# Two-layer cross-attention on one core: where the softmax portions stand beside small projections, which engine copies the fifth and sixth transposes, and when the last weight sums are made

## The chip, the cores and the metric

The kernel runs on one core of a Trainium2 chip. Its time is the device time of one execution in microseconds, median of several runs. The engines that matter here are TensorE (PE in the profile, with its weight loads PEld), VectorE (DVE), ScalarE (ACT), GpSimd (POOL) and SyncE (SP), which issues most loads. Everything is float32.

## The reference

Two cross-attention layers follow each other. There are 8 batches, 100 query rows, 640 channels in 20 heads of 32, and 722 context rows of 1024 channels: the first 77 are "text", the other 645 are "ip". Cut to what matters:

```python
# layer 0
q = split(x @ Wq.T)
out = attend(q, text @ Wk.T, text @ Wv.T) + attend(q, ip @ Wk_ip.T, ip @ Wv_ip.T)
x = out @ Wo.T + bo + x
# layer 1
q = x @ Wq; k_text = text @ Wk; scale = 1 / sqrt(32)
text_out = attend(q, k_text, text @ Wv)
text_probs = softmax(q @ k_text.T * scale)          # over all 640 channels at once
sem = ((text_probs @ text) @ ip.T) * scale          # one row of 645 per query
ip_probs = softmax(scores_ip + 0.5 * sem) * mask
x = (text_out + ip_probs @ ip_v) @ Wout + bout + x
```

`attend` is softmax(q k^T / sqrt(32)) v, per head. The text and the ip part have softmaxes of their own, whose results are added.

## The kernel before

A *unit* u from 0 to 15 is a layer and a batch (u // 8, u % 8); two units make a *pair*. An attention *step* (u, c) is one unit and one chunk c of 128 channels, that is 4 heads. There are 80 steps in `ORDER`: by unit and chunk, except that the last pair goes by groups of chunks, (14,0) (14,2) (15,0) (15,2) (14,1) (14,3) (15,1) (15,3) (14,4) (15,4).

Two streams of work are woven into each other on TensorE.

*Production* makes keys and values of the context, for the pair after the one in attention, and writes them to DRAM, from where each step loads its part. It uses a scheme with seven products in place of eight (`seven`): sums of weights and sums of context blocks are formed first, and results are put together as they leave PSUM. Each task is one product of about 2 us. For the last pair the weights are cut anew: `last_weights` loads them, and `weight_sums` makes four sums, L134 to L137. They are put into the task list of the pair before by `insert` (L1090), at a mark and so many tasks ahead of it: `("k 4", 1, ...)` is one task before the end of that pair's last key products. The first products of the last pair (`psvk`, L736 and L741) read these sums and the block sums `sl` (L232, L233).

*Attention* takes a step in this order. `scores` (L939) computes the logits of one step in two parts (columns 0 to 511, then 512 to 721), takes the maxima on VectorE, and puts the rest of the softmax into a list `later`, as *portions*: `exponentials` (L975, and L993 and L994 with the text part), then `factors` with `scaled_rest(False)` (L997 to L1001, L1015), then two of `scaled` (L1007, two heads each; the first with `scaled_rest(True)`, L1011). `emit(n)` (L931) issues the first n portions. `transposes` (L1036) turns the softmax of the step *before* into six blocks: four transposes into one PSUM tile `pspt` (L1043), then a copy to SBUF, on ScalarE (L1048) or VectorE (L1050). `values` (L1052) multiplies them with v into `pv` and copies the result to `hs` (L1069). Before the first transposes of a step everything in `later` is issued, and so it is before the first scores of a step.

Beside these there are *small* pieces of work, handed out by `small_work(n)`: `out_piece` (output projection, L863, and its addition on VectorE, L868), `q_piece` (queries of layer 1, L882, copied by ScalarE, L886), the `sem_` functions (`sem_text` L836 and L838; `sem_logits` L810 with L815 to L818; `sem_transpose` L823, L825; `sem_scores` L845, L846), and `last_out` (L915). Small pieces, transposes and values all take their PSUM tile from one pool, `ps_pt`, with two buffers: whoever asks waits until the tile two or so before has been read out. In layer 0 output pieces come in steps with c = 1 of even u, in layer 1 the sem pieces of the next unit in steps with c = 3 and 4.

`between(n, a, b, small)` (L1255) weaves one quarter of a step. It runs production tasks up to a point in the plan, sees to it that two things without production between them get a task there (`apart`), and then runs each small piece. Each production task with TensorE work issues one portion before it (`next_task`, L1234), and so does each small piece (L1262).

The order on TensorE, VectorE and ScalarE is fixed: `manual_schedule` (L1225) keeps these three engines in the order in which the program issues. Loads on SP and stores on POOL are placed by the framework. So a line that is issued earlier stands earlier in its engine's queue, whether or not its input is there.

Of the kernel before, what the change touches and what calls it, by code (L numbers as in the profile page):

```python
# [38 lines left out]
PAIRS = [(2 * i, 2 * i + 1) for i in range(NU // 2)]  # L39
# [5 lines left out]
def two_layer_xattn(  # L45
# [47 lines left out]
    def load_quarters(kind, src, n):  # L93

        rows = src.rearrange("(k p) n -> p k n", p=P)
        for i in range(2):
            for j in range(2):
                load_quarter(kind, rows, n, i, j)
# [28 lines left out]
    def weight_sums(kind, n, engines=None):  # L127

        b11, b12, b21, b22 = (W[kind, f"b{x}"] for x in ("11", "12", "21", "22"))
        t2, t3, t4 = (weight_tile(f"w{kind}t{x}", n) for x in (2, 3, 4))  # L130
        W[kind, "t1"], W[kind, "t2"], W[kind, "t3"], W[kind, "t4"] = b12, t2, t3, t4
        first, then = engines or (nc.vector, nc.vector)
        parts = [
            lambda: first.tensor_tensor(t3, b22, b12, ALU.subtract),  # L134
            lambda: first.tensor_tensor(t2, t3, b11, ALU.add),
            lambda: then.tensor_tensor(b12, b12, b11, ALU.subtract),
            lambda: then.tensor_tensor(t4, b21, t2, ALU.subtract),  # L137
        ]
        if engines is None:
            return parts  # L140
        for f in parts:
            f()

    def load_wv(src):
        load_quarters("v", src, HC)
# [5 lines left out]
    def load_wk4(src):  # L151
        W["k", 4] = wpool.tile([P, NCC, P], F32, tag="wk4", name="wk4")
        nc.sync.dma_start(W["k", 4], src.rearrange("(k p) n -> p k n", p=P)[:, :, 4 * P :])
# [299 lines left out]
    def load_q(u):  # L453
        l, b = divmod(u, B)
        t = tpool.tile([P, NC_, S], F32, tag="q", name=f"q_{u}")
        nc.sync.dma_start(t, q_d[l][b // 2][:, b % 2])
        qs_[u] = t
# [471 lines left out]
    later = []  # L929

    def emit(n):  # L931
        for _ in range(n):
            later.pop(0)[1]()
# [102 lines left out]
    def transposes(u, c, j, at_end=False):  # L1036
        if j == 0:
            emit(len(later))
            pts[u, c] = one.tile([P, 6, 4 * S], F32, tag="pt", name=f"pt_{u}_{c}")
        rows = P if j < 5 else NTAIL  # L1040
        ps = ps_pt.tile([P, 512], F32, tag="pt", name=f"pspt_{u}_{c}_{j}")
        for i in range(4):
            nc.tensor.transpose(  # L1043
                ps[:rows, i * S : (i + 1) * S], pr[u, c][:, i, j * P : j * P + rows], ident[:S, :S]
            )
        dst, src = pts[u, c][:rows, j, :], ps[:rows, : 4 * S]
        if j % 3 == 2 or at_end and j == 0:
            nc.scalar.copy(dst, src)  # L1048
        else:
            nc.vector.tensor_copy(dst, src)  # L1050
# [23 lines left out]
    def production():  # L1074

        plan = []
        all_tasks = [pair_tasks(PAIRS[i]) for i in range(1, len(PAIRS) - 1)]
        parts = {}

        def sums_later(kind, n, i):  # L1080
            if kind not in parts:
                parts[kind] = weight_sums(kind, n)
            parts[kind][i]()
            if i == 3:
                del parts[kind]

        def asked(kind, n):
            return [(0.0, lambda i=i: sums_later(kind, n, i)) for i in range(4)]

        def insert(i, *what):  # L1090

            marks = pair_marks[PAIRS[i]]
            for mark, back, tasks in sorted(what, key=lambda w: -(marks[w[0]] - w[1])):
                at = marks[mark] - back
                all_tasks[i - 1][at:at] = tasks


        v, k = asked("v", HC), asked("k", 2 * P)
        insert(
            B // 2 - 1,  # L1100
            ("fifth 4", 0, [(0.0, lambda: load_wk4(wki[1]))]),
            ("v 4", 0, [(0.0, lambda: load_wv(wvi[1]))]),
            ("k 4", 1, v[:1]),
            ("k 4", 0, v[1:2] + [(0.0, lambda: load_quarters("k", wki[1], 2 * P))]),
        )
        insert(
            B // 2,
            ("fifth 0", 1, v[2:3]), ("fifth 0", 0, v[3:]),
            ("fifth 1", 1, k[:1]), ("fifth 1", 0, k[1:2]), ("v 1", 6, k[2:3]), ("v 1", 4, k[3:]),
        )  # L1110

        v_last = asked("v", 2 * P)
        insert(len(PAIRS) - 2, ("v 4", 0, [(0.0, last_weights)]), ("k 4", 1, v_last[:1]), ("k 4", 0, v_last[1:2]))
        for i, tasks in enumerate(all_tasks):
            plan.append((10 * i - AHEAD, 10 * i + 10 - AHEAD, tasks))
        n = 5 * LAST[0]
        every = list(range(NB))
        visits = [(j, lambda j, xs, i, r=r: two_chunks(r, j, xs, i)) for r in range(2) for j in every]
        for kinds, js in (("kv", every[:2]), ("k", every[2:]), ("v", every[2:])):
            visits += [(j, lambda j, xs, i, kinds=kinds: fifth_chunk(kinds, j, xs, i)) for j in js]  # L1120
        lists = last_visits(visits)

        lists[0][5:5] = v_last[2:3]
        lists[0][7:7] = v_last[3:]
        for a, b, tasks in (
            (n - 10 - AHEAD, n + 2.9, lists[: 2 * NB]),
            (n + 2.9, n + 6.9, lists[2 * NB : 3 * NB]),
            (n + 6.9, n + 8.95, lists[3 * NB :]),
        ):
            plan.append((a, b, [t for one_list in tasks for t in one_list]))  # L1130
        return [task for a, b, tasks in plan for task in spread(a, b, tasks)]
# [93 lines left out]
    with tc.manual_schedule(engines={mybir.EngineType.PE, mybir.EngineType.DVE, mybir.EngineType.Activation}):  # L1225
        for _, f in pair_tasks(PAIRS[0]):
            f()
        load_q(0)
        load_vt(0)
        load_k(0, 0)  # L1230
        todo = production()
        done = [0]

        def next_task():  # L1234

            if todo[done[0]][0] and later:
                emit(1)
            todo[done[0]][2]()
            done[0] += 1

        def make(until):
            while done[0] < len(todo) and todo[done[0]][1] < until:
                next_task()

        mark = [0]

        def apart(until):

            while done[0] < len(todo) and todo[done[0]][1] < until and not any(
                t for t, _, _ in todo[mark[0] : done[0]]  # L1250
            ):
                next_task()
            mark[0] = done[0]

        def between(n, a, b, small):  # L1255

            mark[0] = done[0]
            near = 0.4 if n < NC_ * LAST[0] + 6 else 0.1
            for i, (_, f) in enumerate(small):
                make(n + a + (b - a) * (i + 1) / (len(small) + 1))  # L1260
                apart(n + b + near)
                if later:  # L1262
                    emit(1)
                f()
            make(n + b)
            apart(n + b + near)

        make(0.0)
        last = None
        for n, (u, c) in enumerate(ORDER):  # L1270
            at = small_work(n)
            loads(n)
            scores(u, c, 0)
            if n == len(ORDER) - 1:
                load_v(*last)
                load_v(u, c)
            between(n, 0.0, 0.4, at[0])
            if last:
                transposes(*last, 0)
                transposes(*last, 1)  # L1280
            between(n, 0.4, 0.6, at[1])
            if last:
                transposes(*last, 2)
                transposes(*last, 3)
            scores(u, c, 1)
            if n == NC_ * LAST[0] - 1:
                load_q(LAST[1])
            between(n, 0.6, 0.8, at[2])
            if n < len(ORDER) - 2:
                load_v(u, c)  # L1290
            if n + 1 < len(ORDER):
                load_k(*ORDER[n + 1])
            if last:
                transposes(*last, 4)
                transposes(*last, 5)
            between(n, 0.8, 1.0, at[3])
            if last:
                values(*last)
            last = (u, c)
        last_out(0, [NC_ - 1])  # L1300
        for j in range(6):
            transposes(*last, j, at_end=True)
        last_out_add(0)
        values(*last)
        last_out(1, [NC_ - 1])
        last_out_add(1)
# [46 lines left out]
```

## Time and profile before

| what | value |
|---|---|
| median of 3 runs | 2088.91 us (2087.19 to 2090.65) |
| the profiled execution | 2091.22 us, its span 2089.5 us |
| mean granted TensorE clock | 0.995 |
| copies of transposes on VectorE (L1050) | 319, mean 569 ns |
| copies of transposes on ScalarE (L1048) | 161, mean 489 ns |
| VectorE, sum over the span | 1096.1 us |
| ScalarE, sum over the span | 791.4 us |

The span runs from the first instruction to the last; the profiled execution's own time lies 1.7 us above it. TensorE's share of busy time counts modelled ends of matmuls, and a matmul at half clock is busy for longer. In the busy digits of the page TensorE is at 9 tenths in all slices but the last; VectorE and ScalarE are about half busy over the attention. Engines other than TensorE have idle time nearly everywhere, and their busy sums say little: what counts is when a result is there that TensorE waits for.

The lines of a timeline are: start, length, engine, line, operation, output and inputs, shapes, count, and in brackets the idle time of the engine before it with what ended it.

### The profile page before, as it was taken

What the parts mean: (1) busy time and instruction counts of PE and PEld (TensorE: products, weight loads), DVE (VectorE), ACT (ScalarE), POOL (GpSimd) and SP (SyncE); (2) the same over time, 40 slices, a digit from 0 to 9 for tenths busy, and PEclk for the clock granted to TensorE, in tenths of its full rate; (3) what the DMA queues carried; (4) which work ended last, traced back from release to release, by engine and by line L of the source; (5) the groups of instructions that cost most, each with busy time, mean ns of one, the idle gap of its engine ahead of it and who ended that gap; (6) DMA issues with size and microseconds to landing.
All of it is one profiled execution on the core that took longest, in us unless ns stands there. A gap on an engine that the chain in (4) does not pass through costs nothing. (4 is left out here: it accounts for less than half of the span.)

```text
span 2089.5 us, 38492 instructions
## 1 busy us (share of the span) xinstructions
PE 2051.0 (98%) x15122; PEld 1585.3 (76%) x15122; DVE 1096.1 (52%) x2989; ACT 791.4 (38%) x2271; POOL 310.3 (15%) x445
## 2 busy tenths in 40 slices
PE   9999999999999999999999999999999999999998
PEld 8676768677768677776778777787868778888787
DVE  2211222455564555555574655555565556777676
ACT  1001000234343443344333434344444444555576
POOL 3212311111111111010110111101111011111120
PEclk9999999999999999999999999999999999999999
DMA  9545314232424443262634433352425253544382
GB/s 327 157 130 168 93 57 114 84 100 83 120 79 134 119 116 85 87 171 74 175 111 142 120 107 93 91 160 81 122 73 159 75 164 103 161 127 129 110 226 65
DMA packets 302547, 255.38 MB, mean 122 GB/s; under 512 B 46686, under 2 KB 271378, under 8 KB 302366
## 3 DMA queue, kind: packets, MB, share of 16 engines
q1 hardware_dynamic: 280590, 184.48, 32.3%
q0 software_dynamic: 21776, 68.44, 9.5%
q8 instruction: 119, 1.95, 0.4%
q14 instruction: 62, 0.51, 0.1%
HBM read 183.93 MB, written 68.93 MB: 121 GB/s over the span
## 5 line engine op out<-in xcount | busy, mean ns | idle before, releaser
L1050 DVE COPY pt<-pspt 128x400 f32<-128x400 f32 x319 | 175.5, 569 | 135.8 <-PE pspt L1043 133.0
L975 ACT ACTIVATE p<-sc,st 100x512 f32<-100x512 f32 (+1 forms) x320 | 166.0, 531 | 208.2 <-DVE st L961 134.6
L1043 PE MATMUL pspt<-ident,p 100*128 100x100 f32 (+1 forms) x1920 | 214.1, 251 | 24.2 <-DVE res L868 10.9
L1043 PEld LDWEIGHTS pspt<-ident,p 100*128 100x128 f32 (+1 forms) x1920 | 188.7, 137 | 62.8 <-DVE res L868 12.9
L975 ACT ACTIVATE p<-p,st 100x512 f32<-100x512 f32 (+1 forms) x320 | 176.7, 554 | 125.7 <-DVE st L967 125.7
L1007 ACT ACTIVATE p<-p,st 100x512 f32<-100x512 f32 x320 | 208.1, 714 | 42.4 <-DVE st L1001 42.3
L597 PE MATMUL psv_a<-wv,x 128*128 128x397 f32 (+1 forms) x560 | 184.9, 472 | 0.0
L646 POOL DMA_DIRECT2D k_d<-ko x140 | 99.9, 717 | 528.8 <-DVE ko L219 478.6
L597 PE MATMUL psv_d<-wv,s 128*128 128x320 f32 (+1 forms) x560 | 174.9, 455 | 0.0
L1048 ACT COPY pt<-pspt 128x400 f32<-128x400 f32 (+1 forms) x161 | 78.7, 489 | 253.9 <-PE pspt L1043 252.5
L967 DVE CUSTOM_DVE_ANT_0 p<-sc,sem 100x512 f32<-100x512 f32 (+1 forms) x320 | 138.8, 491 | 24.3 <-PE sc L952 24.2
L597 PEld LDWEIGHTS psv_a<-wv,x 128*128 128x128 f32 x560 | 103.5, 189 | 62.1 <-issue 8.1
L597 PEld LDWEIGHTS psv_d<-wv,s 128*128 128x128 f32 x560 | 103.4, 190 | 57.5 <-issue 5.5
L961 DVE TENSOR_REDUCE st<-sc 100x2 f32<-100x1024 f32 (+1 forms) x160 | 125.3, 825 | 30.7 <-PE sc L952 30.7
L952 PE MATMUL sc<-k,q 32*100 32x210 f32 (+1 forms) x1280 | 138.9, 503 | 0.0
L625 PE MATMUL psk_d<-s,wk 128*128 128x256 f32 (+1 forms) x672 | 137.3, 350 | 0.0
L625 PE MATMUL psk_a<-x,wk 128*128 128x256 f32 (+1 forms) x672 | 135.5, 346 | 0.0
L612 POOL DMA_DIRECT2D v_d<-vo x70 | 38.5, 550 | 635.6 <-DVE gst L587 311.5
L563 PE MATMUL psk<-x,wk 128*128 128x256 f32 (+1 forms) x560 | 132.1, 383 | 0.0
L625 PEld LDWEIGHTS psk_a<-x,wk 128*128 128x128 f32 x672 | 109.2, 189 | 20.4 <-issue 6.0
L563 PEld LDWEIGHTS psk<-x,wk 128*128 128x128 f32 x560 | 102.5, 188 | 26.1 <-issue 9.9
L625 PEld LDWEIGHTS psk_d<-s,wk 128*128 128x128 f32 x672 | 108.5, 189 | 17.9 <-issue 5.2
(209 smaller groups left out, 3268.2 us busy)
## 6 DMA issues: line engine op xcount, KB each, us to landing
x<-ip_t SPq DMA_DIRECT2D x84, 512.0 KB
k<-k_d SPq DMA_DIRECT2D x80, 322.5 KB
v<-v_d SPq DMA_DIRECT2D x80, 320.0 KB
v_d<-vo POOLq DMA_DIRECT2D x70, 320.0 KB, 2.5
k_d<-ko POOLq DMA_DIRECT2D x112, 128.0 KB, 4.2
x<-ip_t SPq DMA_DIRECT2D x22, 532.0 KB
o<-wo SPq DMA_DIRECT2D x35, 320.0 KB
q<-wq SPq DMA_DIRECT2D x20, 320.0 KB
```

The source lines that it names most:

```text
L563: nc.tensor.matmul(ps[:, : 2 * n], lhsT=W["k", 4][:, k, :], rhs=x_all[:, at[j], :, k, :n], start=(k == 0), stop=(k == NCC - 1),)
L597: nc.tensor.matmul(ps[:, :m], lhsT=tokens(k)[:, :P], rhs=w[:, k, :], start=(k == 0 and not go_on), stop=(k == HK - 1), skip_group_check=True,)
L625: nc.tensor.matmul(ps[:, i * m : (i + 1) * m], lhsT=W["k", WHICH[which]][:, k, r * P : (r + 1) * P], rhs=tokens(k), start=(i == 0 and k == ...
L646: nc.gpsimd.dma_start(dst[:, :, r], ko[0][:, h, :, i, p0 : p0 + n])
L952: nc.tensor.matmul(scs[i // 2][:S, i % 2, : k1 - k0], lhsT=qs_[u][rows, c, :], rhs=ks[u, c][rows, k0:k1], start=True, stop=True)
L961: nc.vector.tensor_reduce(st[:, part, 2 * h : 2 * h + 2], scs[h][:S, :, :n], AX.X, ALU.max, negate=True)
L967: nc.vector.tensor_tensor_reduce(out=p[:, i, k0 : k0 + n], in0=scs[h][:S, i % 2, :n], in1=sems[u][:, k0 : k0 + n], scale=-1.0, scalar=3.0e ...
L975: nc.scalar.activation(dst, dst if l else scs[h][:S, i % 2, :n], AF.Exp, bias=st[:, part, i : i + 1], scale=-1.0 if l else 1.0, accum_out= ...
L1007: nc.scalar.activation(p[:, i, :KA], p[:, i, :KA], AF.Copy, scale=mul[:, 0, i : i + 1])
L1043: nc.tensor.transpose(ps[:rows, i * S : (i + 1) * S], pr[u, c][:, i, j * P : j * P + rows], ident[:S, :S])
L1048: nc.scalar.copy(dst, src)
L1050: nc.vector.tensor_copy(dst, src)
```

## The change

Three edits. In `between` a small piece no longer issues a portion before itself; portions are issued beside production tasks alone, and where everything is issued. In `transposes` the copies on ScalarE are those of j = 2 and 4, before of j = 2 and 5 (in the last step also j = 0, as before); j = 4 has 128 rows and j = 5 has 82. And the first two weight sums of the last pair are issued one task earlier each: two tasks and one task before the end of the key products, before one and none.

```diff
         dst, src = pts[u, c][:rows, j, :], ps[:rows, : 4 * S]
-        if j % 3 == 2 or at_end and j == 0:
+        if j in (2, 4) or at_end and j == 0:
             nc.scalar.copy(dst, src)
         else:
             nc.vector.tensor_copy(dst, src)
...
         v_last = asked("v", 2 * P)
-        insert(len(PAIRS) - 2, ("v 4", 0, [(0.0, last_weights)]), ("k 4", 1, v_last[:1]), ("k 4", 0, v_last[1:2]))
+        insert(len(PAIRS) - 2, ("v 4", 0, [(0.0, last_weights)]), ("k 4", 2, v_last[:1]), ("k 4", 1, v_last[1:2]))
...
             for i, (_, f) in enumerate(small):
                 make(n + a + (b - a) * (i + 1) / (len(small) + 1))
                 apart(n + b + near)
-                if later:
-                    emit(1)
                 f()
```

In the programs as built, TensorE's order of matmuls is the same before and after. On VectorE and ScalarE some sixty instructions or groups change places, all within their step; on SP five loads of one step change places; POOL's order is the same.

## The prediction

> **What bounds the kernel now.** I read the page's busy line first, then the waits of TensorE alone, then the timeline around its longest waits, then the windows view for the clock.
>
> ```profile
> PE 2051.0 (98%) x15122; PEld 1585.3 (76%) x15122; DVE 1096.1 (52%) x2989; ACT 791.4 (38%) x2271; POOL 310.3 (15%) x445
> ...
> PE pspt L1043 <- DVE res L868: 10.9, 11, 1.9
> PE pspt L1043 <- ACT tp L816: 7.3, 6, 2.7
> PE psq L275 <- DMA wq<-wq: 4.7, 1, 4.7
> PE pspt L1043 <- DVE pt L1050: 2.6, 2, 2.3
> PE psvk_b L736 <- DVE sl L233: 2.5, 1, 2.5
> ```
>
> TensorE is busy 2051.0 of 2089.5 us. Its order of matmuls is the same in both programs as built, so the change can act in only two ways: on the 38 us in which TensorE is not busy, and on the clock it runs at. The waits (line, releaser: us in total, times, longest) name what it waits for: a transposed portion pspt that finds no free PSUM buffer, because the buffer's last user, a small projection (L868) or a logit row (L816), has not been read out. The reader sees how in the timeline of step (11,3):
>
> ```profile
> 1739.40 0.71 DVE L1015 TENSOR_TENSOR p<-p,st 100x532 f32<-100x532 f32 x1
> 1740.03 0.23 DVE L815 TENSOR_REDUCE sst<-psm 100x1 f32<-100x77 f32 x1
> 1740.29 0.33 ACT L816 ACTIVATE tp<-psm,sst 100x77 f32<-100x77 f32 x1 [2.97 <-DVE sst L815]
> ...
> 1740.76 0.54 PE L1043 MATMUL pspt<-ident,p 100*82 100x100 f32 x4 [1.41 <-ACT tp L816]
> ...
> 1741.12 1.22 DVE L135 TENSOR_TENSOR wvt<-wvt,wv 128x1024 f32<-128x1024 f32 x1
> 1742.25 0.69 DVE L232 TENSOR_TENSOR sl<-x 128x512 f32<-128x512 f32 x1
> 1742.97 0.69 DVE L233 TENSOR_TENSOR sl<-sl,x 128x512 f32<-128x512 f32 x1
> 1743.81 0.46 PE L736 MATMUL psvk_b<-wvt,sl 128*128 128x128 f32 x2 [2.50 <-DVE sl L233]
> ```
>
> The logits were done at 1737.2, but L815 stands on VectorE behind the softmax portion L997 to L1015, which itself waited for ScalarE. Last, the windows view (PE, PEld, DVE, ACT, POOL busy, then the granted clock):
>
> ```profile
> 652.02:655.44 3.42, 1.51 (x12) 1.21 (x11) 2.81 (x9) 0.70 (x2) 0.57 (x1) 1.00 0.60 173
> 655.44:658.85 3.41, 3.41 (x11) 3.05 (x10) 0.42 (x1) 2.25 (x4) 0.53 (x1) 0.50 0.00 0
> 1744.29:1747.70 3.41, 3.41 (x30) 3.19 (x33) 1.27 (x3) 0.00 (x0) 0.00 (x0) 0.50 0.00 0
> 1833.04:1839.87 6.83, 6.03 (x64) 5.80 (x68) 2.02 (x7) 3.36 (x7) 0.91 (x2) 0.50 0.41 97
> 1952.50:1959.33 6.83, 5.97 (x60) 3.80 (x64) 3.27 (x12) 4.38 (x10) 0.00 (x0) 0.50 0.07 24
> ```
>
> After four of the long waits TensorE runs at half clock for 3.4 or 6.8 us, and counts as busy there. A wait can cost more than its own length.
>
> **What the Trainium skill says.** "TensorE: Matmul & The Clock Gate", Part 1, says that TensorE's clock goes to half after an idle window of about 3.4 us, counted in free-running windows. The windows above agree on half rate and the 3413 ns step. On the trigger the trace differs: a wait of 1.91 us inside one window (652.25 to 654.16) was enough, while equal waits at 892 and 1127, which by that 3413 ns grid straddle a boundary, were followed by full clock. The same page ("Engine queue depths") says that VectorE and ScalarE take their queues strictly in order; the timeline agrees, L815 waits though its input is there.
>
> **The change, part by part.** Times are of before's execution.
>
> *No portion beside small projections, waits of L868.* In steps (2,1), (4,1), (6,1), (8,1), (12,1) and (14,2) the fourth L868 moves ahead of L997 to L1015. It then starts 0.2 us after its matmuls, as it does elsewhere, where the wait left is 0.18 us. So 3 x (1.91 - 0.18) + (1.47 - 0.18) + (1.41 - 0.18) + (1.39 - 0.18) = 8.9 us.
>
> *Waits of L816.* In the p = 3 steps L815 moves ahead of the portion, and L816 ahead of L1007. The waits at 1284 (1.14), 1517 (0.70) and 1919 (0.89) go fully. At 1833 (2.71) L815 still follows L731 and L213, which ends at 1831.30: L815 0.23, L816 0.33 and two handovers of 0.1 give 1831.9 against a natural 1831.13, so 0.75 stays and 1.96 goes. Sum 4.7 us.
>
> *Two products sooner.* L134 (1.22) now stands before the evacuation L219 at 1733.11, before which VectorE idles 1.96 us, so it is hidden if its weights have landed. They were issued by 1718.1, and the DMA share falls to near nothing between 1724 and 1727; if they had not, SP's queue would stall VectorE there. L135 then starts at 1736.65 in L134's old place. Chain: L135 to 1737.87, L224 to 1738.21, L815 and L816 to 1738.73, L817 and L818 to 1739.30, L232 and L233 to 1740.64, psvk_b at 1740.8 instead of 1743.81. Both waits at this place (1.41 and 2.50) shrink by 3.0 us together; about 1.0 stays.
>
> *Smaller ones.* L838 at 1821.98 moves between two pairs of exponentials: 0.47. At 1953.36 the sixth transposes now get another buffer, freed by L825, which moves from 1953.32 to about 1951.0 because the exponentials of (14,0) go behind it: 2.27 goes, but the second sem product waits for L846 of the first, about 0.5 (bounds 0 and 0.9): 1.8.
>
> *Clock.* All four half-rate windows follow waits that go or fall to 1.0 or less, and no wait of 1.67 us inside a window (the one at 892) set one off. TensorE was busy 3.41 + 3.41 + 6.03 + 5.97 = 18.8 us in them; half is 9.4. Checked by start-to-start times: from the sixth transposes to the next scores 6.27 us (1833.84 to 1840.11) against 3.45 for the same sequence at 1919.58 to 1923.03, 2.8 lost where the half gives 3.0. I take 8.8; bounds 5 (two windows come back elsewhere, the grid being free-running) and 9.4.
>
> *Fifth transposes.* It is a swap: 80 copies of 128x400 go to ScalarE and 80 of 82x400 to VectorE. The timeline has 0.57 on VectorE and 0.49 on ScalarE for either, so no engine gains work. What moves is the release: the fifth's buffer is free without VectorE's softmax, but the last four matmuls of pv now need VectorE's copy. Usually a product of about 2 us lies between the sixth transposes and pv and covers that copy. In the closing steps, with waits of 0.58 and 0.65 at 2060 to 2062, I count 0.3 gained. Cost without cover: up to the 0.57 of a copy in a step.
>
> *Portions later.* L1007 and L1011 end up to 4 us later. In before they end 6 to 13 us ahead of the next step's first transposes up to step (11,3), 2 to 7 after it, and 4.6 in (14,2), where the delay is about 3: covered. The closing steps before the last one have almost none, but their order stays. L193, L202 and L886 pass ahead of L1007, which helps PSUM. SP only swaps a few loads, POOL's order is the same.
>
> *What it costs at the end.* In the last step the final copy of pv, L1069, now stands ahead of L997 to L1011:
>
> ```profile
> 2074.13 0.46 DVE L997 TENSOR_REDUCE st<-p 100x4 f32<-100x308 f32 x1
> 2075.45 2.56 ACT L1007 ACTIVATE p<-p,st 100x512 f32<-100x512 f32 x4 [0.99 <-DVE st L1001]
> 2077.41 0.26 DVE L1069 COPY hs<-pv 128x100 f32<-128x100 f32 x1 [1.31 <-PE pv L1065]
> 2078.93 0.85 PE L1043 MATMUL pspt<-ident,p 100*128 100x100 f32 x8
> ```
>
> L1069 can't start before 2077.41. From it to the first L1007 takes 1.5 us in the step before (2062.61 to 2064.12), so L1007 runs from 2078.9 to 2081.5, one head each 0.62. The first transposes, at 2078.93 in before, wait for heads one by one and end near 2081.7 instead of 2079.4: 2.3 us lost, all on the path. Half clock after it would add up to 1.
>
> Sum: 8.9 + 4.7 + 3.0 + 0.5 + 1.8 + 8.8 + 0.3 - 2.3 = 25.7 us off the span: 2089.5 - 25.7 = 2063.8, and with the 1.7 us around the span (2091.22 - 2089.5) 2065.5. The profiled execution lies 2.3 above the median of 2088.91, perhaps with one or two half-rate windows more than the others; from the median the same sum gives 2063.2. I take 2064.5.
>
> **Rivals.** (1) *The clock does not follow.* The waits go, but what stays (0.18, 0.75, 1.0, the new 2.3) sets off as many half-rate windows. For: the trigger is known from four cases only. Against: no single wait left in mid-kernel is over 1.1. Only the waits then count: 2088.9 - 16.9 = 2072. (2) *The wait is replaced.* Only the L868 waits go, since the reduction L815 holds up the portion behind L816's answer, and TensorE waits at the next pspt instead: 8.9 and one window, about 2078. Against: slack of 6 us and more. (3) *Slower.* VectorE's copy of the sixth transposes stands behind the 2.0 us of L997 to L1015 in the p = 3 steps and comes 0.5 later than the fifth's everywhere, and pv needs it. If pv waited longer than the 28 us gained over 80 steps less the 2.3, that is over 0.32 us in each step, the kernel would be slower; at 0.5 each, 2103. For: the wait of 0.65 at 2061.99 is of this kind. Against: pv reads that copy last, 0.9 us after it starts, and in nearly all steps a product comes first. (4) *Nothing happens*, the order being made good elsewhere: 2089. Against: the order as built does move.
>
> **How the numbers follow.** Forecast 0.74 with its own range 2060.5 to 2069 (2.3 or 0 at the end, clock 5 to 9.4, median or profiled base); rival 1 0.12; rival 2 0.06; rival 3 0.05; rival 4 0.03. Reaching towards rival 1, the range is 2060 to 2072. A measurement of this kernel can tell some 0.2% (4 us) from no change: faster 0.92, same 0.03, slower 0.05.
>
> **What would show it.** In the changed profile: pspt waiting for L868 near 1.3 us in total instead of 10.9, for L816 near 1.2; psvk_b for L233 near 1.0; hardly any half-rate clock before the end; a new group, pspt waiting for p L1007, of about 2.3 us more. L868 waits still of 1.4 and more, a VectorE wait of some us at L134, or pv waiting for pt L1050 in many steps would prove me wrong.

## The result, and the profile after

The changed kernel takes 2067.68 us (median of 4 runs, 2067.52 to 2068.61), the kernel before beside it 2089.02 (4 runs, 2087.19 to 2090.65): a ratio of 0.9899, 95% interval 0.9882 to 0.9916. The forecast was 2064.5, with a range of 2060 to 2072. The profiled execution took 2067.52 us, its span 2065.8, at a mean granted TensorE clock of 0.998.

The page's busy line and the waits of TensorE in the changed kernel (what waits, its line, the releaser, then us in total, times, longest):

```profile
PE 2043.4 (99%) x15122; PEld 1579.3 (76%) x15122; DVE 1096.4 (53%) x2989; ACT 793.5 (38%) x2271; POOL 309.1 (15%) x445
...
PE psq L275 <- DMA wq<-wq: 4.2, 1, 4.2
PE pspt L1043 <- ACT p L1007: 3.0, 9, 0.6
PE pspt L1043 <- DVE res L868: 2.9, 11, 1.2
...
PE pspt L1043 <- ACT tp L816: 1.2, 2, 0.8
PE psvk_b L736 <- DVE sl L233: 1.1, 1, 1.1
```

Three things are to be seen. The waits for L868 fell from 10.9 to 2.9 and those for L816 from 7.3 to 1.2, but one L868 wait is 1.2 us long, and it is a new one. L1007 rose from 1.5 (five waits of 0.3) to 3.0. And TensorE does the same 15122 instructions with 7.6 us less busy time: that is mostly the clock, since a matmul at half clock counts as busy for longer (the products L625 at 656 of before start 0.43 us apart at half clock, and 0.22 apart in the changed kernel).

How the first kind of wait went is seen in the timeline of step (2,1), first in the kernel before:

```profile
651.74 0.51 PE L1043 MATMUL pspt<-ident,p 100*128 100x100 f32 x4
651.78 0.47 DVE L997 TENSOR_REDUCE st<-p 100x4 f32<-100x308 f32 x1 [0.92 <-ACT p L994]
...
653.06 0.71 DVE L1015 TENSOR_TENSOR p<-p,st 100x532 f32<-100x532 f32 x1
653.69 0.42 DVE L868 SCALAR_TENSOR_TENSOR res<-pso,bias_sb,res 128x200 f32<-128x200 f32 x1
...
654.16 0.54 PE L1043 MATMUL pspt<-ident,p 100*82 100x100 f32 x4 [1.91 <-DVE res L868]
```

Then in the changed kernel:

```profile
651.22 0.51 PE L1043 MATMUL pspt<-ident,p 100*128 100x100 f32 x4
651.42 0.42 DVE L868 SCALAR_TENSOR_TENSOR res<-pso,bias_sb,res 128x200 f32<-128x200 f32 x1 [1.08 <-PE pso L863]
651.90 0.54 PE L1043 MATMUL pspt<-ident,p 100*82 100x100 f32 x4 [0.17 <-DVE res L868]
...
652.97 0.46 DVE L997 TENSOR_REDUCE st<-p 100x4 f32<-100x308 f32 x1
...
654.24 0.71 DVE L1015 TENSOR_TENSOR p<-p,st 100x532 f32<-100x532 f32 x1
```

L868 now stands ahead of the softmax portion L997 to L1015, starts as soon as its product is done, and the sixth transposes wait 0.17 us for it and no longer 1.91. In step (11,3) the logits go ahead in the same way (timeline of the changed kernel):

```profile
1725.57 1.22 DVE L135 TENSOR_TENSOR wvt<-wvt,wv 128x1024 f32<-128x1024 f32 x1
1727.05 0.23 DVE L815 TENSOR_REDUCE sst<-psm 100x1 f32<-100x77 f32 x1
1727.31 0.33 ACT L816 ACTIVATE tp<-psm,sst 100x77 f32<-100x77 f32 x1 [1.06 <-DVE sst L815]
1727.77 0.85 PE L1043 MATMUL pspt<-ident,p 100*128 100x100 f32 x8
...
1728.85 0.69 DVE L233 TENSOR_TENSOR sl<-sl,x 128x512 f32<-128x512 f32 x1
1729.69 1.13 PE L736 MATMUL psvk_b<-wvt,sl 128*128 128x128 f32 x8 [1.06 <-DVE sl L233]
1730.73 0.71 DVE L1015 TENSOR_TENSOR p<-p,st 100x532 f32<-100x532 f32 x1
```

The eight transposes run without a break, psvk_b waits 1.06 instead of 2.50, and L1015 comes last instead of first.

Two things were lost again. One is a new wait in (14,2). In the kernel before, ScalarE made the exponentials of (14,0) ahead of both L846, and L868 waited for nothing but its product (timeline of before):

```profile
1950.77 0.41 ACT L975 ACTIVATE p<-p,st 100x133 f32<-100x133 f32 x1 [1.15 <-DVE st L967]
...
1955.36 0.44 ACT L846 ACTIVATE sem<-psm 100x323 f32<-100x323 f32 x1 [0.59 <-PE psm L845]
...
1963.72 0.42 DVE L868 SCALAR_TENSOR_TENSOR res<-pso,bias_sb,res 128x200 f32<-128x200 f32 x1 [0.19 <-PE pso L863]
```

And in the changed kernel:

```profile
1929.69 0.44 ACT L846 ACTIVATE sem<-psm 100x322 f32<-100x322 f32 x1 [0.88 <-PE psm L845]
1930.03 0.40 ACT L975 ACTIVATE p<-p,st 100x133 f32<-100x133 f32 x1
...
1932.17 0.47 DVE L997 TENSOR_REDUCE st<-p 100x4 f32<-100x308 f32 x1 [1.01 <-ACT p L994]
...
1937.87 0.75 DVE L868 SCALAR_TENSOR_TENSOR res<-pso,bias_sb,res 128x200 f32<-128x200 f32 x2
1938.43 0.88 PE L1043 MATMUL pspt<-ident,p 100*128 100x100 f32 x8 [1.18 <-DVE res L868]
1939.63 1.96 PE L863 MATMUL pso<-hs,o 128*128 128x200 f32 x10 [0.32 <-DVE pt L1050]
```

The exponentials of (14,0) now stand on ScalarE behind both L846, although their input was there at 1928.7 (L990 started at 1928.54 and took 0.17). So L997 starts at 1932.17, the maxima of the next scores and L730 and L198 follow it in VectorE's queue, and L868 comes at the end of this chain. The other loss is in the last step. The changed kernel's timeline there and its windows (us, busy of PE, PEld, DVE, ACT, POOL, granted clock, DMA share, GB/s):

```profile
2049.26 0.26 DVE L1069 COPY hs<-pv 128x100 f32<-128x100 f32 x1 [2.86 <-PE pv L1065]
2049.44 0.46 DVE L997 TENSOR_REDUCE st<-p 100x4 f32<-100x308 f32 x1
...
2050.77 2.56 ACT L1007 ACTIVATE p<-p,st 100x512 f32<-100x512 f32 x4 [2.78 <-DVE st L1001]
2051.54 0.31 PE L1043 MATMUL pspt<-ident,p 100*128 100x100 f32 x1 [0.60 <-ACT p L1007]
2052.15 0.30 PE L1043 MATMUL pspt<-ident,p 100*128 100x100 f32 x1 [0.31 <-ACT p L1007]
```

```profile
1813.30:1820.13 6.83, 6.02 (x90) 4.95 (x90) 5.46 (x19) 4.02 (x9) 1.43 (x2) 1.00 0.80 199
...
2049.44:2052.85 3.41, 2.05 (x13) 1.55 (x13) 2.23 (x8) 2.08 (x4) 0.00 (x0) 1.00 0.00 0
2052.85:2059.68 6.83, 6.60 (x70) 5.12 (x70) 2.31 (x4) 1.95 (x4) 0.00 (x0) 0.50 0.01 2
```

L1069 stands ahead of L997, L1007 runs from 2050.77 to 2053.33, and the first transposes wait for its heads one by one. After that TensorE runs at half clock for 6.83 us. The first of the three windows starts at the wait that took 2.71 us before: 0.81 us of it are left, and the clock stays full.

Because the order of TensorE's 15122 instructions is the same, the nth of one execution can be set beside the nth of the other, and the shift of its start read between any two points. From the profiled executions, in us of gain, each figure rounded by itself:

| place | prediction | measured |
|---|---|---|
| six L868 waits: (2,1), (4,1), (6,1), (8,1), (12,1), (14,2) | 8.9 | 1.7 + 1.7 + 1.7 + 1.3 + 1.2 + 1.2 = 8.9 |
| L816 at 1284, 1517, 1833, 1919 of before | 4.7 | 1.2 + 0.9 + 2.0 + 1.1 = 5.2 |
| step (11,3), both waits | 3.0 | 2.9 |
| L838 | 0.5 | 0.7 |
| sixth transposes of (14,0) | 1.8 | 1.6 |
| clock: shift less waits at 655, 1744, 1833, 1952 of before | 8.8 | 1.7 + 1.9 + 2.8 + 2.4 = 8.8 |
| closing steps but the last | 0.3 | 0.2 |
| (14,2): new waits | 0 | -1.4 |
| last step | -2.3 | -4.5 |
| rest: the start 0.5, and small shifts of 0.1 to 0.3 | | 1.3 |
| span | 25.7 | 23.7 |

### The profile page after: what moved, and what is told of

Its sections match the earlier page's. It is cut to its first block, busy times and chain, and to the rows that moved or that the text cites. A ratio compares the mean times of both kernels' runs of the same rounds, so it can differ in the third digit from the quotient of the medians.

```text
span 2065.8 us, 38497 instructions
## 1 busy us (share of the span) xinstructions
PE 2043.4 (99%) x15122; PEld 1579.3 (76%) x15122; DVE 1096.4 (53%) x2989; ACT 793.5 (38%) x2271; POOL 309.1 (15%) x445
## 4 chain that ended last, share of the span: by engine, by line
PE 97%; DVE 2%; ACT 1%; issue 0%; DMA 0%; SPq 0%; DVEq 0%; ACTq 0%
PE psv_a L597 8%; PE psv_d L597 8%; PE pspt L1043 8%; PE psk_a L625 6%; PE psk L563 6%; PE psk_d L625 6%; PE sc L952 6%; PE pv L1065 5%; PE psv_e L597 4%; PE psv_c L597 4%; PE psv_b L597 4%; PE psk_e L625 3%; PE psk_b L625 3%; PE psk_c L625 3%; PE pso L863 3%; PE psq L275 2%
## 5 line engine op out<-in xcount | busy, mean ns | idle before, releaser
L1050 DVE COPY pt<-pspt 128x400 f32<-128x400 f32 (+1 forms) x319 | 175.2, 569 | 147.6 <-PE pspt L1043 146.3
L1007 ACT ACTIVATE p<-p,st 100x512 f32<-100x512 f32 x320 | 207.5, 713 | 58.6 <-DVE st L1001 58.4
L1048 ACT COPY pt<-pspt 128x400 f32<-128x400 f32 x161 | 79.3, 493 | 252.1 <-PE pspt L1043 251.9
L625 PE MATMUL psk_d<-s,wk 128*128 128x256 f32 (+1 forms) x672 | 136.4, 348 | 0.0
L625 PE MATMUL psk_a<-x,wk 128*128 128x256 f32 (+1 forms) x672 | 135.5, 346 | 0.0
L625 PEld LDWEIGHTS psk_a<-x,wk 128*128 128x128 f32 x672 | 109.2, 189 | 20.4 <-issue 6.0
L625 PEld LDWEIGHTS psk_d<-s,wk 128*128 128x128 f32 x672 | 108.1, 189 | 17.8 <-issue 5.2
```

Source lines behind the costliest of these rows:

```text
L625: nc.tensor.matmul(ps[:, i * m : (i + 1) * m], lhsT=W["k", WHICH[which]][:, k, r * P : (r + 1) * P], rhs=tokens(k), start=(i == 0 and k == ...
L1007: nc.scalar.activation(p[:, i, :KA], p[:, i, :KA], AF.Copy, scale=mul[:, 0, i : i + 1])
```

## The experiments

Each run stands beside runs of the kernel before on the same chip: for the first four their median is 2090.27 (25 runs, 2086.08 to 2093.88), for the other four 2089.81 (9 runs, 2085.72 to 2091.16).

**Edit 1 alone, on the kernel before.**

```diff
                 apart(n + b + near)
-                if later:
-                    emit(1)
                 f()
```

> The first edit alone on the kernel before: no portion beside small pieces, copies of j = 2 and 5 on ScalarE, weight sums where they were. My theory (the waits of L868 and L816, and the clock that follows them, are nearly all of the gain): about 20 us faster than before, 2068 to 2070; waits of pspt for L868 near 2.9 us in total, for L816 near 1.2; psvk_b for L233 near 2 us, since L135 now stands between L818 and L232. Rival (which engine copies the fifth transposes decides, because it frees the PSUM buffer): under 8 us faster. Rival (the half-rate windows are chance): half-rate windows as many as in before, some 13 us faster.

2071.66 us (5 runs, 2070.06 to 2072.1), ratio 0.9914 (0.9901 to 0.9928). L816 1.2 and psvk_b 2.2 are as expected; L868 is 1.9, where 2.9 was expected. The wait of 1.2 us at (14,2) is missing (0.17 is left): in this execution TensorE ran at half clock from 1931.42 to 1934.83, in (14,0), and so came to the transposes of (14,2) later, when L868 was done. Up to the last step the execution is 25.0 us ahead of the one before; there 5.0 come back, since TensorE runs at half clock from 2057.71 to the end, 11.8 us. So edit 1 alone gives 18.6 us where the three give 21.3, and its cost at the end varies with the clock (5.0 here, 4.5 in the changed kernel).

**Edit 2 alone: the swap of the fifth and sixth copies.**

```diff
-        if j % 3 == 2 or at_end and j == 0:
+        if j in (2, 4) or at_end and j == 0:
```

> The second edit alone on the kernel before: j = 2 and 4 on ScalarE. My theory: between 1 us faster and 1 us slower; all waits for L868 and L816 as in before (10.9 and 7.3). Rival (the swap frees the buffers): 10 us faster or more. Rival of the other side (the values product waits for VectorE's copy of the sixth transposes): 5 us slower or more, with pv waiting for pt L1050 in many steps.

2082.6 us (5 runs, 2081.21 to 2083.33), ratio 0.9966 (0.9954 to 0.9979): my expectation was wrong by 7 us. Its waits of TensorE, and then its timeline at (2,1):

```profile
PE pspt L1043 <- ACT tp L816: 7.3, 6, 2.7
...
PE pspt L1043 <- ACT pt L1048: 3.7, 7, 0.6
...
PE pspt L1043 <- DVE res L868: 0.9, 5, 0.2
```

```profile
652.27 0.51 PE L1043 MATMUL pspt<-ident,p 100*128 100x100 f32 x4
652.82 0.49 ACT L1048 COPY pt<-pspt 128x400 f32<-128x400 f32 x1 [0.55 <-PE pspt L1043]
653.37 0.54 PE L1043 MATMUL pspt<-ident,p 100*82 100x100 f32 x4 [0.58 <-ACT pt L1048]
654.22 0.42 DVE L868 SCALAR_TENSOR_TENSOR res<-pso,bias_sb,res 128x200 f32<-128x200 f32 x1
```

L868 is as late as before, but the sixth transposes no longer wait for it. They wait 0.58 us for L1048, the copy of the *fifth* transposes. The pool has two buffers. The tile of the sixth transposes now takes the fifth's, where before it took the projection's; the semaphore for which that matmul waits is one of ScalarE's in this kernel and one of VectorE's before. So the next buffer isn't given by strict rotation. In the three kernels looked at here it is the one whose reader ends first: L868 before (654.11, L1050 at 654.58), L868 in the changed kernel (651.84, L1048 at 652.25), and L1048 in this one (653.31, L868 at 654.64). That this is the rule is read from these three and wasn't tried by itself. What the run shows is that the choice of the copying engine moves a wait from one line to another. The gain at each of the six places is 0.8 to 1.3 us, and at 655 the half clock (1.7) is gone too. In (14,0) the wait moves as well, from L1050 (2.3) to L825 (2.5), and nothing is gained.

**Edit 3 alone: the first two weight sums one task sooner each.**

```diff
-... ("k 4", 1, v_last[:1]), ("k 4", 0, v_last[1:2]))
+... ("k 4", 2, v_last[:1]), ("k 4", 1, v_last[1:2]))
```

> The third edit alone on the kernel before: the first two weight sums of the last pair one product earlier each. My theory: psvk_b waits about 1.3 us for L233 in place of 2.5, and the half-rate window behind it may go: 1.2 to 2.9 us faster. Rival (the weights have not landed at the earlier place): VectorE stands at L134 and the kernel is 0 to 3 us slower.

2088.52 us (21 runs, 2082.1 to 2093.09), ratio 0.9988 (0.9979 to 0.9997). psvk_b waits 1.4 instead of 2.5; L868 (10.9) and L816 (7.3) are untouched. The gain of 1.8 us in the median is as expected, but barely clear of the spread, and the spread is the finding: one program, 11 us apart, and over its 21 runs the mean granted clock falls as the time rises (0.999 in the run of 2082.1, 0.993 in that of 2092.95). The profiled execution was one of the short ones, span 2080.6. Windows of 8 us around the wait at (2,1), first this run, then the kernel before:

```profile
650.00:658.00 8.00, 6.09 (x37) 5.57 (x37) 4.04 (x12) 3.95 (x11) 2.72 (x4) 1.00 0.27 78
```

```profile
651.00:659.00 8.00, 6.09 (x29) 5.40 (x28) 3.48 (x10) 3.70 (x9) 2.12 (x3) 0.79 0.26 74
```

The same wait of 1.91 us, the same busy time, but 37 matmuls in the window against 29. The shift between the two executions is 1.7 us here and 2.8 at the wait of 1833, with equal waits: this is the price of the half clock by itself, near what the prediction took from half of the busy time (1.7 and 3.0).

**The changed kernel with one portion beside each small piece of the last step again.**

```diff
                 apart(n + b + near)
+                if later and n == len(ORDER) - 1:
+                    emit(1)
                 f()
```

> The changed kernel, but in the last step small pieces issue a portion before themselves as in before, so that L997 to L1015 stand ahead of L1069 again. My theory: the wait of pspt for p L1007 at the end goes, and the half-rate window that starts there too: 4.3 us faster than the changed kernel, 2063.4, span near 2061.5. Rival (only the wait goes, the half clock at the end comes anyway): 2.3 us faster, 2065.4. Rival (the end is set by the copies of the last transposes): under 1 us faster.

2063.1 us (4 runs, 2062.76 to 2063.65), ratio 0.9875 (0.9861 to 0.9888), span 2061.9 at a clock of 1.0. Its timeline at the end:

```profile
2048.17 2.56 ACT L1007 ACTIVATE p<-p,st 100x512 f32<-100x512 f32 x4 [1.55 <-DVE st L1001]
2048.48 1.06 PE L1065 MATMUL pv<-pt,v 128*32 128x100 f32 x40
...
2049.79 0.26 DVE L1069 COPY hs<-pv 128x100 f32<-128x100 f32 x1 [0.96 <-PE pv L1065]
...
2051.30 0.85 PE L1043 MATMUL pspt<-ident,p 100*128 100x100 f32 x8
```

L1007 begins 1.6 us before L1069 and not 1.5 after it, the transposes run in one piece, and the last step costs what it did before, to 0.05 us. The median lies 4.6 us under the changed kernel's: the loss in the last step was this order, wait and half clock together.

**One more portion put back, between the two score products of step (14,0).**

```diff
-                if later and n == len(ORDER) - 1:
+                if later and (n == len(ORDER) - 1 or n == NC_ * LAST[0] and a == 0.8 and i == 1):
                     emit(1)
```

> The last-step version (e4) with one more portion put back: in step (14,0), between the two score products of the text half, so that ScalarE makes the exponentials of (14,0) between the two L846 instead of behind both. Theory: the 1.36 us given back at (14,2) is a chain on ScalarE and VectorE (both L846, exponentials until 1932.1, L997 to L1011, four L967, L730, L198, then L868), and it starts 1.15 us too late. The two waits there (1.18 for L868, 0.32 for pt L1050) shrink to 0.2 and 0.3, total pspt<-L868 from 2.9 to 1.9, time 2061.9 (1.0 to 1.3 under e4's 2063.1). Rival: the second L846, now behind the exponentials, holds its buffer 1.6 us longer and a wait comes there instead; then the same time as e4 or up to 0.5 slower.

2061.56 us (4 runs, 2061.11 to 2061.99), ratio 0.987 (0.9857 to 0.9883). L868 is at 1.7 in total with 0.2 the longest. Its timeline at (14,2), where the run before waited 1.18:

```profile
1940.23 0.56 PE L1043 MATMUL pspt<-ident,p 100*128 100x100 f32 x4 [0.17 <-DVE res L868]
```

Matmul by matmul, 1.1 us are gained between (14,0) and (14,2) against the run before. The chain on ScalarE was the cause; the second L846, now behind the exponentials, delays nobody.

**That, and the first two weight sums one task sooner again.**

```diff
-... ("k 4", 2, v_last[:1]), ("k 4", 1, v_last[1:2]))
+... ("k 4", 3, v_last[:1]), ("k 4", 2, v_last[1:2]))
```

> As e5, with the last pair's first two weight sums one product sooner again (three and two products before the mark). Theory: psvk_b stands 1.06 us for L233 because L135 (1.22) lies right before the chain L224, L815 to L818, L232, L233; one product sooner it lies under a product, behind L213, where L134 lies now. The wait goes to about 0, and the 0.43 for tp L816 in the same step as well: 1.0 to 1.4 us under e5, 2060.7. Rival: the weights have not landed when L134 now comes up (about 1717.5 on the changed kernel's clock), VectorE stands there, and its copy L1050 and then TensorE wait up to 2 us: 2062 or more.

2060.34 us (4 runs, 2059.42 to 2061.51), ratio 0.9864 (0.9851 to 0.9878). This is better than both kernels, 7.3 us under the changed one, with an interval of the ratio that lies wholly below that one's. Its timeline at (11,2) and (11,3):

```profile
1717.48 1.21 DVE L134 TENSOR_TENSOR wvt<-wv,wv 128x1024 f32<-128x1024 f32 x1
1718.69 0.43 DVE L213 TENSOR_TENSOR ko<-psk_d,ko 128x266 f32<-128x266 f32 x1
1719.04 1.21 DVE L135 TENSOR_TENSOR wvt<-wvt,wv 128x1024 f32<-128x1024 f32 x1
...
1727.84 1.13 PE L736 MATMUL psvk_b<-wvt,sl 128*128 128x128 f32 x8 [0.17 <-DVE sl L233]
```

L134 starts without a wait, so its weights had landed by then, and psvk_b waits 0.17 instead of 1.06; matmul by matmul that is 0.9 us. The waits for L816 stayed at 1.2. The one of 0.43 us, which I had put into the same step, stands in (14,0) (at 1923.32 in this run), where these sums have no part.

**Edit 1 beside the small projections alone, on the kernel before.** In the second and third of each five steps of `ORDER` (c = 1 and 2, and for the last pair (14,2), (15,0), (15,1) and (15,3)) a small piece issues no portion; beside the sem pieces and in the last step it does, as before.

```diff
-                if later:
+                if later and n % NC_ not in (1, 2):
                     emit(1)
```

> Edit 1 alone and only beside the small projections (out_piece, q_piece): before without a portion there, everything else as before. Theory: the L868 waits go from 10.9 to about 1.9 and nothing else moves: L816 stays 7.3, psvk_b 2.5, the last step keeps 1.5 for p L1007. 9 us of waits and the half-rate window at 655, 1.7, where it comes: 2080 (2077 to 2082), near what the swap alone gave (2082.6), since both free the same buffer for the sixth transposes. The other half-rate windows may come or not by phase. Rival: the gain of the swap has another source, then this one and the swap differ by more than 5 us.

2079.2 us (5 runs, 2077.55 to 2079.42), ratio 0.9953 (0.9941 to 0.9966). L868 1.9, L816 7.2, psvk_b 2.5: as expected. So of edit 1's 18.6 us 10.6 come from the projections, and the rest, 8.0, would be what the text pieces bring less the loss in the last step, if the two parts of edit 1 add.

**The last-step version with the swap undone.**

```diff
-        if j in (2, 4) or at_end and j == 0:
+        if j % 3 == 2 or at_end and j == 0:
```

> The last-step version (e4) with the swap of the fifth and sixth copies undone (fifth on VectorE, sixth on ScalarE as before). Theory: the swap's 7.7 us alone were the L868 waits of the sixth transposes, which edit 1 removes by itself; with edit 1 in place the swap is worth little. L868 waits about 2 to 3, and 0.3 to 1.0 more for the sem product behind a copy of ScalarE and for pv: 2063.7 (2063.1 to 2064.5). Rival: the swap adds its 7.7 to edit 1 in full: about 2071.

2064.31 us (4 runs, 2062.34 to 2064.82), ratio 0.9881 (0.9866 to 0.9896), against 2063.1 for the version with the swap. With edit 1 in place the swap is worth about 1 us, and the ranges of the runs overlap. Between the profiled executions it is 0.8 us of span. Of this 0.4 lies in the sem product of (14,0), which waits 0.6 for a copy of ScalarE where it waited 0.2, and the rest in shifts of at most 0.2, pv of a closing step among them.

## Why the prediction came out as it did

*Waits of L868 (8.9) and of L816 (4.7).* Right in mechanism and in size, 8.9 and 5.2. The rule used, that the line starts 0.2 us after its matmuls and 0.17 to 0.18 us of wait stays, is what the changed timeline shows. The Trainium skill, "TensorE: Matmul & The Clock Gate" (Engine queue depths), has VectorE and ScalarE take their queues strictly in order. The traces agree: in (2,1) L868 has its product by 651.9 and starts at 653.69, behind the portion, where in the changed kernel it starts at 651.42, ahead of it; and the loss at (14,2) comes the same way. Rival 2, that TensorE waits at the next pspt instead, falls with L816's 1.2 us.

*Step (11,3) (3.0).* Right: 2.9, and 1.06 us stays where "about 1.0" was said. The run with sums alone shows the two edits' shares: 1.1 from the sums, the rest from L815 going ahead.

*Clock (8.8).* Right in size in mid-kernel, and shown: the run with the sums alone has the same waits at 655 and 1833 without half clock, and gains 1.7 and 2.8 there. Rival 1, that the clock doesn't follow, falls with the mean clock of 0.998 and the full rate at all four places. One reading beside it doesn't hold. That 1.67 us inside a window set nothing off was taken as a safe size, but the half rate at 1952.50 in before began in the middle of its wait of 2.27 us, after a window with 1.62 us of idle time in all. So the length of idle time alone doesn't decide below 1.9 us.

*The end (-2.3, and "half clock after it would add up to 1").* Here the prediction was off. The wait was right: matmul by matmul, the shift of the first transposes grows over their four heads to 2.3 us at the fourth, which starts at 2053.38 where L1007 ends at 2053.33. (In the list of waits only 1.5 us of it appear, 3.0 against 1.5 for L1007, since the lone transposes count 0.3 us each as busy.) The half clock after it is the term that was mis-sized: over the rest of the matmuls the loss goes on from 2.3 to 4.3, so the clock took 2.0 us, twice the bound given. The four runs of the changed kernel have mean clocks of 0.997 to 0.998 and lie within 1.1 us, so the profiled execution is no exception. I had put it beside the sum and not in it, though the same text took a half-rate window to follow waits of this length elsewhere. The last-step version shows the whole 4.6 us.

*Portions later ("4.6 in (14,2), where the delay is about 3: covered").* Right for the readers of the portion, and wrong as the whole account. In (14,2) of the changed kernel L1007 ends at 1952.39 and the transposes that read it start at 1955.55, so they are covered. But the next to be late is not a reader of the portion: it is L868, which in (14,2) stands behind the portion of (14,0), the next maxima, L730 and L198 in VectorE's queue. The prediction put this at nothing. It cost 1.4 us, and putting the exponentials between the two L846 brings 1.1 of it back.

*The swap (0.3).* Right as a sum, since it stands beside edit 1, and wrong as a picture: "what moves is the release" was seen, but not that the sixth transposes could then take the fifth's buffer. Alone the swap gains 7.7 us in the median. In its profiled execution 6.5 us of gain lie at the same six L868 waits that edit 1 cuts, and 1.7 in the half clock at 655. The parts alone give 18.6 + 7.7 + 1.8 = 28.1 us, the whole 21.3. Rival 3, that pv waits for VectorE's sixth copy, shows in one place only: 0.8 us for L1050, as much in total as before.

*The base.* The sum gave 2065.5 from the profiled execution and 2063.2 from the median, and I took 2064.5. The profiled execution measured 2067.5: 2.0 over, nearly all of it the clock in the last step. The smaller misses, -1.4 at (14,2) against 0.5 more at L816 and 1.3 of small shifts, cancel, and that is luck. Leaning towards the median cost the third microsecond: the time before in that profile was 2.3 us above its median, and the changed kernel has none of this excess to lose.

## What to carry to other kernels

In this kernel short reads that free a shared PSUM buffer belonged ahead of long softmax portions in an in-order queue, but move a portion back and every line behind it in that queue moves too: look for the next buffer that one of those lines frees, not only for the portion's readers. Count a wait of TensorE together with the half clock that it may set off, at the end of the kernel as well as in the middle. And test edits alone and left out: two edits may remove the same wait, and then their gains don't add.

## What the runs showed of the hardware

From the ten profiled executions: in each of them all changes of TensorE's clock lie on one grid of 3413.33 ns, within 2.2 ns, as the Trainium skill has it ("TensorE: Matmul & The Clock Gate", Part 1: free-running windows of 4096 cycles at 1.2 GHz). The idle time inside one grid window against what the next window's clock was:

```
idle of TensorE in one 3.413 us window     windows   next at half clock
1.89 us and more (1.894 to 2.716)              9          9
1.10 to 1.78 us                               32          5
```

(Windows that were themselves at half clock are left out, and so is the last whole window of each execution, whose next one is cut off by the end; with these it would be 15 of 15 and 7 of 35. No window with less idle time was followed by half clock.) The page speaks of an idle window of about 3.4 us; here 1.9 us out of 3.4 was always enough. The five below, at 1.11 to 1.62 us, all lie in step (14,0) or in the last step; why these and not the others was not tried.

The grid doesn't start with the kernel: in the ten executions the clock first becomes full between 7.7 and 10.8 us after the first instruction. So the same wait falls into one window or is cut in two. The wait of 1.91 us lay wholly in one window in the kernel before, and with 1.78 us in the run with the sums alone, and the 1.7 us of half clock followed in the first only. This fits the spread of 11 us between runs of one program, whose clock goes with their time; but of those 21 runs one alone has a trace, so that the phase makes the whole spread is not shown. Nor do long waits always bring such a spread: the swap alone and the run with edit 1 beside the projections keep waits of 2.7 us and repeat within 2.1 and 1.9 us (5 runs each), about as closely as the versions without them (0.9 to 2.5 us, 4 runs each).
